# Carrying each answer's destination with its token: the last mixture-of-experts layer of a four-layer graph network

## The chip, the cores and the metric

The kernel runs on one core of a Trainium2 chip. The core has a matrix engine (PE, with its weight loads shown apart as PEld), a vector engine (DVE), an activation engine (ACT), a general engine (POOL, or GpSimd) and a queue engine (SP). DMA transfers are issued from SP, ACT and POOL and are carried by 16 DMA engines that all of them share. Transfers with a list of row numbers (gathers and scatters) are issued from POOL here.

The metric is the device time of one execution in microseconds (us). Before the change it is 6287.54 us, the median of nine runs from 6260.56 to 6317.55 us.

## The reference

3125 nodes with 256 features pass through four layers. Each layer adds a graph layer and a feed-forward layer to x, each applied to a layer norm of x. Only the last feed-forward layer concerns us. It is a mixture of 8 experts of which each token uses the best two:

```python
gate_logits = xf @ Wg + bg
top_w, top_i = jax.lax.top_k(gate_logits, TOP_K)          # TOP_K = 2 of E = 8
top_w = jax.nn.softmax(top_w, axis=-1)
w_dense = jnp.sum(jax.nn.one_hot(top_i, E, dtype=xf.dtype) * top_w[..., None], axis=1)
out = jnp.zeros_like(xf)
for e in range(E):
    h = jax.nn.gelu(xf @ W1[e] + b1[e], approximate=False)  # 256 -> 1024
    out = out + w_dense[:, e:e + 1] * (h @ W2[e] + b2[e])   # 1024 -> 256
```

Then x = x + out, and that is the kernel's output. A token is a node.

## The kernel before

The nodes are kept in an order of the kernel's own, padded to NP = 3200, as NT = 25 tiles of P = 128 rows of D = 256 numbers. X holds all of x in on-chip memory ([128, 25, 256]), XNH holds its layer norm with eight columns to spare ([128, 25, 264]), and XN is the first 256 columns of XNH. `pid(g)` is the list of the nodes' places in the output.

The last feed-forward layer does not compute all experts for all tokens. It sorts the 2 x 3200 choices by expert:

1. *Places* (L1518, `expert_places`). Each choice gets a row, `top_pos`, in a table `top_in` in device memory. The rows of one expert start at a multiple of R3 = 256, so that the table falls into T3 = 32 tiles of 256 rows, each of a single expert. 32 x 256 = 8192 rows hold 6400 choices; the rest stay at zero, which `cleared` (L1503) wrote long before, from the tile `zeros`, while the gates of an earlier layer were computed.
2. *Scatter in.* 50 scatters of 128 rows each (one per node tile and choice, by the helper at L1083) write the normed tokens into `top_in`. They are on POOL.
3. *Turns* (L1575, `in_turns`). For each tile j there are four steps, in a software pipeline written out by hand: in turn s the kernel does `given_back3(s-3)`, `hidden3(s-2)`, `turn_rows3(s-1)` and `load3(s)`, in that order. The order on every engine is the order in which they are written (a manual schedule).
   - `load3` loads the tile's 256 tokens (xq, on ACT's queue) and the weights and biases of the tile's expert (w1, b1, w2, b2, 1 MB each for w1 and w2, on SP's queue).
   - `turn_rows3` transposes the tokens on PE into ft_ps (L2900) and copies them out on DVE (xt, L2901).
   - `hidden3` multiplies by W1 on PE (fh_ps, L2909, 32 matmuls) and applies the GELU on ACT (ht, L2911).
   - `given_back3` multiplies by W2 on PE (fo_ps, L2921, 32 matmuls), adds the bias on DVE (ys, L2923) and writes the 256 answers as a plain block of `top_out`, a table of 8192 rows in the order of `top_in` (L2924, on SP's queue).
4. *The end* (L2928 to L2933). For each of 25 node tiles and each of the two choices, a gather by `top_pos` fetches the answers from `top_out` into y (POOL, helper at L1079, eight buffers), and DVE adds gate times y to X (L2932). A scatter by `pid(g)` then writes X[:, g, :] to the output (POOL, helper at L1083). Rows past the last node are dropped by a bounds check.

The helper `scatter` declares the scatters into one table free of dependences among themselves, because each has rows of its own. Readers of the table wait for the scatters that wrote it.

Of the kernel before, what the change touches and what calls it, by code (L numbers as in the profile page):

```python
# [11 lines left out]
F32 = mybir.dt.float32  # L12
BF16 = mybir.dt.bfloat16
I32 = mybir.dt.int32
AF = mybir.ActivationFunctionType
ALU = mybir.AluOpType
# [4 lines left out]
P = 128  # L21
D = 256
KD = D // P
N = 3125
NT = (N + P - 1) // P
NP = NT * P
# [1029 lines left out]
BATCH = 5  # L1056
# [13 lines left out]
W1 = D + 1  # L1070
# [7 lines left out]
def gather(nc, out_, table, idx):  # L1078
    return nc.gpsimd.indirect_dma_start(out=out_, out_offset=None, in_=table, in_offset=index(idx))  # L1079


def scatter(tc, group, table, idx, in_, **bounds):
    s = tc.nc.gpsimd.indirect_dma_start(out=table, out_offset=index(idx), in_=in_, in_offset=None, **bounds)  # L1083
    tc.declare_no_dep(s.ins, group=group, reason="each node has a row of its own")
    tc.add_to_no_dep_group(group, s.ins)
# [328 lines left out]
def quick(ctx: ExitStack, tc: tile.TileContext, a: dict, out: bass.AP, k):  # L1414
# [3 lines left out]
    nc, dram, ident, ones = tc.nc, k.dram, k.ident, k.ones  # L1418
    q = ctx.enter_context(tc.tile_pool(name="q", bufs=1))
    X = q.tile([P, NT, D], F32, name="X")  # L1420
    XNT = q.tile([P, KD, NP], F32, name="XNT")
    f = parts(tc, a, k, X, XNT)
# [8 lines left out]
    slot = q.tile([P, KS[0]], F32, name="slot")  # L1431
    nc.gpsimd.iota(slot, pattern=[[1, KS[0]]], base=0, channel_multiplier=0,
                   allow_small_or_imprecise_dtypes=True)
    zeros = q.tile([P, D], F32, name="zeros")
    nc.vector.memset(zeros, 0.0)
    zero = zeros[0:1, :]

    def pid(g):
        return PRi[:, g, 0:1]
# [7 lines left out]
    def batches():  # L1447
        return [range(b, b + BATCH) for b in range(0, NT, BATCH)]
# [44 lines left out]
            pass  # L1493


    def token_tables(name, choices, n_exp, rows):


        T = (choices * NP + n_exp * (rows - 1)) // rows
        tin, tout = (dram.tile([T * rows, D], F32, name=f"{name}_{s}") for s in ("in", "out"))  # L1500
        return T, tin, tout

    def cleared(tin):  # L1503

        r = tin.shape[0] // P
        for i in range(0, r, 8):
            n = min(8, r - i)
            nc.sync.dma_start(tin[i * P : (i + n) * P, :].rearrange("(r p) d -> p r d", p=P),
                              zeros[:, None, :].to_broadcast([P, n, D]))
            yield 0  # L1510

    SWE, SWH = 32, 64
    sw_T, sw_in, sw_out = token_tables("sw", 1, SWE, P)
    E3, F3, R3 = 8, 1024, 2 * P
    FC3 = F3 // P
    T3, top_in, top_out = token_tables("top", 2, E3, R3)

    def expert_places(pool, psum, ohs, n_exp, rows, T, pos_i):  # L1518

# [55 lines left out]
    def in_turns(T, steps, beside=None, pace=None):  # L1575


        with tc.manual_schedule():
            for s in range(T + max(d for _, d in steps)):
                for step, d in steps[::-1]:  # L1580
                    if 0 <= s - d < T:
                        step(s - d)
                if beside:
                    for _ in range(pace(s)):
                        next(beside, None)
            if beside:
                for _ in beside:
                    pass
# [127 lines left out]
    for g in range(NT):  # L1716
        w = min(10, P // KS[g])
        n = -(-P // w)
# [11 lines left out]
    with tc.tile_pool(name="ep", bufs=1) as pool:  # L1730
        NJ = max(n for _, n, _ in TILES)
        firsts = pool.tile([P, NT, NJ], F32, name="ep_first")
        for g, (w, _, _) in enumerate(TILES):
            nc.gpsimd.iota(firsts[:, g, :], pattern=[[w, NJ]], base=w, channel_multiplier=0,
                           allow_small_or_imprecise_dtypes=True)
# [4 lines left out]
        t = t_at  # L1740
# [244 lines left out]
    with tc.tile_pool(name="gg", bufs=gbufs) as gp, tc.tile_pool(name="gm", bufs=3) as mp, \  # L1985
# [5 lines left out]
        b2 = f.row(a["L0_gnn_b2"], D, wp, "b2")  # L1991
# [75 lines left out]
    with tc.tile_pool(name="rt", bufs=1) as rt_pool:  # L2067
# [8 lines left out]
        with tc.tile_pool(name="sc", bufs=1) as sc:  # L2076
# [24 lines left out]
            with tc.tile_pool(name="tkp", bufs=1, space=PSUM) as tkp, tc.tile_pool(name="sk", bufs=2) as sk:  # L2101
# [4 lines left out]
                for c0, n in CHUNKS:  # L2106
                    xmt = sk.tile([P, PP, 512], F32, name="xmt")
                    for c in range(PP):
                        ps = tkp.tile([P, 512], F32, name="xm_ps", bufs=2)
# [4 lines left out]
                    for i in range(n // P):  # L2114
                        t = c0 // P + i
# [4 lines left out]
                        sw = SW[:, t, :].rearrange("p (h g) -> p h g", h=H)  # L2120
# [8 lines left out]
                        fx = fxs[t % 2]  # L2129
# [724 lines left out]
    with tc.tile_pool(name="fc", bufs=1) as fc, tc.tile_pool(name="fw", bufs=2) as fw, \  # L2854
            tc.tile_pool(name="fx", bufs=2) as fx, tc.tile_pool(name="fps", bufs=2, space=PSUM) as fps:
        iota_e = f.places(fc, E3)
        ms_, ohs = [], []
        for i in range(2):
            m_ = fc.tile([P, NT], F32, name=f"top{i}")
            nc.vector.tensor_reduce(m_, lg3, AX.X, ALU.max)  # L2860
            o = f.first_of(fc, lg3, m_, iota_e, E3, f"top{i}_oh")
            if i == 0:
                nc.vector.scalar_tensor_tensor(lg3, o, -BIG, lg3, op0=ALU.mult, op1=ALU.add)
            ms_.append(m_)
            ohs.append(o)
        pos = fc.tile([P, 2 * NT], I32, name="top_pos")
        win = expert_places(fc, fps, ohs, E3, R3, T3, pos)
        for i in range(2 * NT):
            scatter(tc, "top_in", top_in, pos[:, i : i + 1], XN[:, i % NT, :])
        gate = fc.tile([P, 2, NT], F32, name="gate")  # L2870
        nc.vector.tensor_sub(gate[:, 1, :], ms_[1], ms_[0])
        nc.scalar.activation(gate[:, 1, :], gate[:, 1, :], AF.Exp)
        nc.vector.tensor_scalar_add(gate[:, 0, :], gate[:, 1, :], 1.0)
        nc.vector.reciprocal(gate[:, 0, :], gate[:, 0, :])
        nc.vector.tensor_mul(gate[:, 1, :], gate[:, 1, :], gate[:, 0, :])
        ld, xt, ht = {}, {}, {}
        regs = {}

        def load3(j):
            if j % WG == 0:  # L2880
                regs["e"] = experts_at(win, j, E3)
            e = bass.ds(regs["e"][j % WG], 1)
            xq = fx.tile([P, 2, D], F32, name="xq")
            nc.scalar.dma_start(xq, top_in[j * R3 : (j + 1) * R3, :].rearrange("(i p) d -> p i d", p=P))
            w1 = fw.tile([P, KD, F3], F32, name="w1")
            nc.sync.dma_start(w1, a["L3_ffn_W1"][e, :, :].rearrange("a (k p) h -> p (a k) h", p=P))
            b1 = fx.tile([P, FC3], F32, name="b1t", bufs=3)
            nc.sync.dma_start(b1, b1t[e, :, :].rearrange("a p f -> p (a f)"))
            w2 = fw.tile([P, FC3, D], F32, name="w2", bufs=3)
            nc.sync.dma_start(w2, a["L3_ffn_W2"][e, :, :].rearrange("a (f p) d -> p (a f) d", p=P))  # L2890
            b2 = fx.tile([P, D], F32, name="b2t", bufs=3)
            nc.sync.dma_start(b2, a["L3_ffn_b2"][e, :].to_broadcast([P, D]))
            ld[j] = xq, w1, b1, w2, b2

        def turn_rows3(j):
            xt[j] = fx.tile([P, KD, R3], F32, name="xt")
            ps = fps.tile([P, KD, R3], F32, name="ft_ps", bufs=1)
            for c in range(KD):
                for i in range(2):
                    nc.tensor.transpose(ps[:, c, i * P : (i + 1) * P], ld[j][0][:, i, c * P : (c + 1) * P], ident)  # L2900
            nc.vector.tensor_copy(xt[j], ps)  # L2901

        def hidden3(j):
            ht[j] = fx.tile([P, FC3, R3], F32, name="ht")
            for f_ in range(0, FC3, 2):
                ps = fps.tile([P, 2, R3], F32, name="fh_ps", bufs=3)
                for i in range(2):
                    for c in range(KD):
                        nc.tensor.matmul(ps[:, i, :], ld[j][1][:, c, (f_ + i) * P : (f_ + i + 1) * P], xt[j][:, c, :],  # L2909
                                         start=(c == 0), stop=(c == KD - 1))  # L2910
                    nc.scalar.activation(ht[j][:, f_ + i, :], ps[:, i, :], AF.Gelu, bias=ld[j][2][:, f_ + i : f_ + i + 1])  # L2911
            xt.pop(j)

        def given_back3(j):
            _, _, _, w2, b2 = ld.pop(j)
            h = ht.pop(j)
            ys = fx.tile([P, 2, D], F32, name="ys")
            ps = fps.tile([P, 2, D], F32, name="fo_ps")
            for i in range(2):
                for f_ in range(FC3):  # L2920
                    nc.tensor.matmul(ps[:, i, :], h[:, f_, i * P : (i + 1) * P], w2[:, f_, :],  # L2921
                                     start=(f_ == 0), stop=(f_ == FC3 - 1))
            nc.vector.tensor_add(ys, ps, b2[:, None, :].to_broadcast([P, 2, D]))  # L2923
            nc.sync.dma_start(top_out[j * R3 : (j + 1) * R3, :].rearrange("(i p) d -> p i d", p=P), ys)  # L2924

        in_turns(T3, ((load3, 0), (turn_rows3, 1), (hidden3, 2), (given_back3, 3)))

        for g in range(NT):  # L2928
            for i in range(2):
                y = fx.tile([P, D], F32, name="y", bufs=8)  # L2930
                gather(nc, y, top_out, pos[:, i * NT + g : i * NT + g + 1])
                nc.vector.scalar_tensor_tensor(X[:, g, :], y, gate[:, i, g : g + 1], X[:, g, :],  # L2932
                                               op0=ALU.mult, op1=ALU.add)  # L2933
            scatter(tc, "out", out, pid(g), X[:, g, :], bounds_check=N - 1, oob_is_err=False)


@with_exitstack
# [60 lines left out]
```

## Time and profile before

The profile shows one execution. Its span, from the first to the last instruction, is 6286.5 us; the execution took 6287.92 us.

| what | number |
|---|---|
| median of nine runs | 6287.54 us |
| the profiled execution, its span | 6287.92 us, 6286.5 us |
| busy over the whole span: PE, DVE, ACT, POOL | 60%, 50%, 19%, 50% |
| granted PE clock over the span (1 is full speed) | 0.758 |
| first and last start of the scatters into `top_in` | 5535.80, 5598.51 us |
| first PE instruction of the expert tiles (ft_ps) | 5603.72 us |
| last ys on DVE (L2923) | 6177.49 us, for 0.69 us |
| first gather of y, last scatter to the output | 6181.49 us, 6277.53 us |
| gathers of y | 50, mean 0.960 us |
| scatters to the output | 25, mean 1.019 us |
| DVE at the end (L2932) | 50, mean 0.484 us |

How to read it: an instruction is named by its line, its engine and out<-in, with the names of the tiles. A line of a helper (L1079 gather, L1083 scatter) appears for many tiles, so the tile's name tells which it is. The idle time before an instruction is put down to what ended it: "<-DMA y" means that the engine waited for a transfer of y, "<-issue" that the profile shows nothing that it waited for. A PE that is busy is not always at full clock; the windows give the granted clock. The chain of waits is followed back from the last instruction, and an engine outside of it may idle at no cost.

### The profile page before, as it was taken

The numbers are of one execution on the slowest core, as the hardware profiler recorded it, in microseconds if no ns is written. First come the engines' busy times: TensorE is split into PE (matmuls) and PEld (weight loads), VectorE is DVE, ScalarE is ACT, GpSimd is POOL, SyncE is SP. The second block draws the span as 40 slices with busy tenths as digits, with TensorE's granted clock in tenths as the row PEclk, the third lists the DMA queues.
The fourth block names the chain that finished last, engine by engine and source line by source line (L and its number), as shares of the span: only waits on it lengthen the run. The fifth ranks groups of instructions, "written<-read, shape, count | busy, mean of one in ns | idle before, by whom it ended". The sixth has DMA issues, their size and how long they took to land. (4 is left out here: it accounts for less than half of the span.)

```text
span 6286.5 us, 45072 instructions
## 1 busy us (share of the span) xinstructions
PE 3784.4 (60%) x14067; PEld 2484.4 (40%) x14119; DVE 3123.7 (50%) x6023; ACT 1222.0 (19%) x2574; POOL 3128.5 (50%) x3044
## 2 busy tenths in 40 slices
PE   2245533455598844535286712889676688838882
PEld 2233332333355423423153411556342344436662
DVE  4578868898874345601153426333224677810001
ACT  1222212445532100000042411110120000012220
POOL 4677774677773266676467573110126566430004
PEclk9667666667799956656598855999656787769996
DMA  4534442333312233222242214332243233234442
GB/s 128 136 96 107 107 109 81 91 92 100 90 23 83 112 91 91 78 74 56 60 147 68 73 38 121 109 110 95 80 117 85 81 88 86 65 109 158 158 159 84
DMA packets 357953, 602.95 MB, mean 96 GB/s; under 512 B 109331, under 2 KB 254331, under 8 KB 354370
## 3 DMA queue, kind: packets, MB, share of 16 engines
q0 software_dynamic: 130800, 329.16, 19.9%
q1 hardware_dynamic: 207657, 251.79, 12.5%
q10 hardware_dynamic: 19238, 18.93, 0.9%
q8 instruction: 116, 1.90, 0.1%
q14 instruction: 142, 1.16, 0.1%
HBM read 458.77 MB, written 142.93 MB: 96 GB/s over the span
## 5 line engine op out<-in xcount | busy, mean ns | idle before, releaser
L1620 PE MATMUL acc<-wv,ident 128*128 128x256 f32 x2818 | 923.6, 488 | 631.7 <-ACT wv L1632 264.8
L1079 POOL DMA_INDIRECT gt<-T,recs x906 | 1013.9, 1119 | 365.2 <-issue 247.7
L1620 PEld LDWEIGHTS acc<-wv,ident 128*128 128x128 f32 x2818 | 662.8, 246 | 893.1 <-ACT wv L1632 297.3
L1079 POOL DMA_INDIRECT gt<-TA,recs x453 | 454.8, 1004 | 259.4 <-issue 127.3
L1079 POOL DMA_INDIRECT gt<-gm,recs x428 | 478.2, 1117 | 180.8 <-issue 128.7
L1079 POOL DMA_INDIRECT gt<-rel,relz x453 | 443.0, 978 | 208.8 <-issue 126.9
L1705 PE MATMUL acc<-gt,ident 128*128 128x256 f32 x906 | 320.0, 485 | 209.1 <-issue 168.2
L2566 PE MATMUL acc<-XNT,adj_g 128*128 128x512 bf16 x1198 | 402.2, 384 | 42.0 <-ACT XNT L2558 42.0
L2797 PE MATMUL e_ps<-EW,att 32*128 32x512 f32 (+7 forms) x466 | 296.7, 764 | 145.8 <-ACT att L2787 106.4
L1672 ACT ACTIVATE m<-m 128x1024 f32<-128x1024 f32 (+2 forms) x258 | 256.5, 994 | 630.7 <-DVE m L1671 370.6
L2569 PE MATMUL acc<-F,adj_g 128*128 128x256 bf16 x1250 | 343.4, 275 | 9.3 <-DVE F L2559 6.6
L1079 POOL DMA_INDIRECT y<-top_out,top_pos x50 | 48.0, 960 | 596.9 <-issue 595.7
L1671 DVE TENSOR_TENSOR m<-gt,R 128x1028 f32<-128x1028 f32 (+4 forms) x258 | 297.0, 1151 | 89.5 <-DMA gt<-T,recs 87.5
L1705 PEld LDWEIGHTS acc<-gt,ident 128*128 128x128 f32 x906 | 205.8, 239 | 303.8 <-issue 196.2
L2909 PE MATMUL fh_ps<-xt,w 128*128 128x256 f32 x1024 | 266.9, 399 | 76.2 <-ACT ht L2911 75.4
L1677 DVE TENSOR_TENSOR m<-m,att 128x1024 f32<-128x1024 f32 (+2 forms) x258 | 294.2, 1140 | 28.0 <-issue 28.0
L1634 DVE TENSOR_TENSOR wv<-gt,L 128x1024 f32<-128x1024 f32 (+3 forms) x252 | 285.2, 1136 | 43.2 <-remote 39.1
L1678 DVE TENSOR_REDUCE L<-m 128x4 f32<-128x1024 f32 (+4 forms) x258 | 294.3, 1141 | 11.2 <-DVE m L1677 3.3
L2438 PE MATMUL x_ps<-XNT,x_w 128*128 128x512 f32 (+1 forms) x448 | 223.6, 633 | 100.8 <-ACT x_h L2440 74.3
L2909 PEld LDWEIGHTS fh_ps<-xt,w 128*128 128x128 f32 x1024 | 187.7, 193 | 150.3 <-ACT ht L2911 128.1
L2459 DVE TENSOR_TENSOR x_y<-x_o,x_b 128x512 f32<-128x512 f32 (+1 forms) x52 | 34.4, 669 | 416.1 <-remote 256.4
L2452 PE MATMUL x_o<-x_w,x_h 128*128 128x256 f32 x800 | 204.7, 401 | 50.4 <-issue 25.7
(557 smaller groups left out, 6603.7 us busy)
## 6 DMA issues: line engine op xcount, KB each, us to landing
w<-in_L_ffn_W_dram SPq DMA_DIRECT2D x64, 1024.0 KB
adj_g<-adj SPq DMA_DIRECT2D x50, 800.0 KB
adj<-em_a SPq DMA_DIRECT2D x25, 800.0 KB
gt<-T,recs POOLq DMA_INDIRECT x906
y<-each_d SPq DMA_DIRECT2D x25, 512.0 KB
each_d<-x_y SPq DMA_DIRECT2D x24, 512.0 KB
R<-rr SPq DMA_DIRECT2D x25, 388.0 KB
top_in<-zeros SPq DMA_DIRECT2D x8, 1024.0 KB
```

Source lines behind the costliest of these rows:

```text
L1079: return nc.gpsimd.indirect_dma_start(out=out_, out_offset=None, in_=table, in_offset=index(idx))
L1620: nc.tensor.matmul(acc, ident, wv[:, s, :], start=(c + s == 0), stop=(c + s == K - 1))
L1634: nc.vector.tensor_mul(wv[:, :n, :].rearrange("p s (h c) -> p s h c", h=H), t[:, :n, :D].rearrange("p s (h c) -> p s h c", h=H), L[:, c : ...
L1671: nc.vector.tensor_add(m[:, :n, :], st[g].tiles[c][:, :n, :], st[g].R[:, 1:2, :].to_broadcast([P, n, W]))
L1672: nc.scalar.activation(m[:, :n, :D], m[:, :n, :D], AF.Abs)
L1677: nc.vector.tensor_mul(m[:, :n, :D], m[:, :n, :D], att[:, None, :].to_broadcast([P, n, D]))
L1678: nc.vector.tensor_reduce(L, m[:, :n, :D].rearrange("p s (h c) -> p s h c", h=H), AX.X, ALU.add)
L1705: nc.tensor.matmul(accs[g], ident, t[:, s, :], start=False, stop=(last and s == n - 1))
L2566: nc.tensor.matmul(acc.rearrange("p s d -> p (s d)"), A[:, b, :], F12[:, b, :, :].rearrange("p s d -> p (s d)"), start=(b == 0), stop=Fals ...
L2569: nc.tensor.matmul(acc[:, 0, :], A[:, b, :], F3_[:, b, :], start=False, stop=(b == NT - 1), skip_group_check=True)
L2797: nc.tensor.matmul(e_ps[:, :z, :].rearrange("p s d -> p (s d)"), att, EW[: att.shape[0], s0 : s0 + z, :].rearrange("p s d -> p (s d)"), st ...
L2909: nc.tensor.matmul(ps[:, i, :], ld[j][1][:, c, (f_ + i) * P : (f_ + i + 1) * P], xt[j][:, c, :], start=(c == 0), stop=(c == KD - 1))
```

## The change

`top_out` becomes a table in the order of the nodes: row n for the first choice of node n, row 3200 + n for its second, 6400 rows in all. Each token carries the row of its answer with it:

- Rows of `top_in` have 257 numbers instead of 256; the last is the destination less 8192 (OUTSIDE). `zeros` and the clearing writes are 257 wide as well, so that a row that holds no token has a zero there, hence the destination 8192, which is past the table's end.
- The column behind XN in XNH is set to the row of the first choice (an iota on POOL, a copy on DVE). After each of the first 25 scatters into `top_in` DVE sets it to the row of the second choice for that tile, which it can do only when the scatter has read it.
- xq is 257 wide. After the copy xt, DVE turns the last column into the integers `to` ([128, 2] for a tile).
- `given_back3` no longer writes `top_out`. Two new steps of the turn, `send(0)` and `send(1)`, scatter the two halves of ys to `top_out` by `to`, with a bounds check that drops the destination 8192. Each is followed on POOL by a memset of a one-number tile, `mark`. ys has three buffers instead of two.
- The end has no gathers. For each of five batches of five node tiles, two plain loads of 640 KB (one on SP's queue with the first choice's rows, one on ACT's with the second's) bring the answers into y, with two buffers. The 50 DVE operations and the 25 scatters to the output stay.

```diff
--- before.py
+++ after.py
@@ -1431,9 +1431,9 @@
     slot = q.tile([P, KS[0]], F32, name="slot")
     nc.gpsimd.iota(slot, pattern=[[1, KS[0]]], base=0, channel_multiplier=0,
                    allow_small_or_imprecise_dtypes=True)
-    zeros = q.tile([P, D], F32, name="zeros")
+    zeros = q.tile([P, W1], F32, name="zeros")
     nc.vector.memset(zeros, 0.0)
-    zero = zeros[0:1, :]
+    zero = zeros[0:1, :D]
 
     def pid(g):
         return PRi[:, g, 0:1]
@@ -1493,12 +1493,11 @@
             pass
 
 
-    def token_tables(name, choices, n_exp, rows):
+    def token_table(name, choices, n_exp, rows, width):
 
 
         T = (choices * NP + n_exp * (rows - 1)) // rows
-        tin, tout = (dram.tile([T * rows, D], F32, name=f"{name}_{s}") for s in ("in", "out"))
-        return T, tin, tout
+        return T, dram.tile([T * rows, width], F32, name=name)
 
     def cleared(tin):
 
@@ -1506,14 +1505,18 @@
         for i in range(0, r, 8):
             n = min(8, r - i)
             nc.sync.dma_start(tin[i * P : (i + n) * P, :].rearrange("(r p) d -> p r d", p=P),
-                              zeros[:, None, :].to_broadcast([P, n, D]))
+                              zeros[:, None, : tin.shape[1]].to_broadcast([P, n, tin.shape[1]]))
             yield 0
 
     SWE, SWH = 32, 64
-    sw_T, sw_in, sw_out = token_tables("sw", 1, SWE, P)
+    sw_T, sw_in = token_table("sw_in", 1, SWE, P, D)
+    sw_out = dram.tile([sw_T * P, D], F32, name="sw_out")
     E3, F3, R3 = 8, 1024, 2 * P
     FC3 = F3 // P
-    T3, top_in, top_out = token_tables("top", 2, E3, R3)
+
+    OUTSIDE = 8192
+    T3, top_in = token_table("top_in", 2, E3, R3, W1)
+    top_out = dram.tile([2 * NP, D], F32, name="top_out")
 
     def expert_places(pool, psum, ohs, n_exp, rows, T, pos_i):
 
@@ -2865,22 +2868,29 @@
             ohs.append(o)
         pos = fc.tile([P, 2 * NT], I32, name="top_pos")
         win = expert_places(fc, fps, ohs, E3, R3, T3, pos)
+        node = fc.tile([P, NT], F32, name="node")
+        nc.gpsimd.iota(node, pattern=[[P, NT]], base=-OUTSIDE, channel_multiplier=1,
+                       allow_small_or_imprecise_dtypes=True)
+        nc.vector.tensor_copy(XNH[:, :, D], node)
         for i in range(2 * NT):
-            scatter(tc, "top_in", top_in, pos[:, i : i + 1], XN[:, i % NT, :])
+            g = i % NT
+            scatter(tc, "top_in", top_in, pos[:, i : i + 1], XNH[:, g, :W1])
+            if i < NT:
+                nc.vector.tensor_scalar_add(XNH[:, g, D:W1], node[:, g : g + 1], float(NP))
         gate = fc.tile([P, 2, NT], F32, name="gate")
         nc.vector.tensor_sub(gate[:, 1, :], ms_[1], ms_[0])
         nc.scalar.activation(gate[:, 1, :], gate[:, 1, :], AF.Exp)
         nc.vector.tensor_scalar_add(gate[:, 0, :], gate[:, 1, :], 1.0)
         nc.vector.reciprocal(gate[:, 0, :], gate[:, 0, :])
         nc.vector.tensor_mul(gate[:, 1, :], gate[:, 1, :], gate[:, 0, :])
-        ld, xt, ht = {}, {}, {}
+        ld, xt, ht, ys, to = {}, {}, {}, {}, {}
         regs = {}
 
         def load3(j):
             if j % WG == 0:
                 regs["e"] = experts_at(win, j, E3)
             e = bass.ds(regs["e"][j % WG], 1)
-            xq = fx.tile([P, 2, D], F32, name="xq")
+            xq = fx.tile([P, 2, W1], F32, name="xq")
             nc.scalar.dma_start(xq, top_in[j * R3 : (j + 1) * R3, :].rearrange("(i p) d -> p i d", p=P))
             w1 = fw.tile([P, KD, F3], F32, name="w1")
             nc.sync.dma_start(w1, a["L3_ffn_W1"][e, :, :].rearrange("a (k p) h -> p (a k) h", p=P))
@@ -2899,6 +2909,8 @@
                 for i in range(2):
                     nc.tensor.transpose(ps[:, c, i * P : (i + 1) * P], ld[j][0][:, i, c * P : (c + 1) * P], ident)
             nc.vector.tensor_copy(xt[j], ps)
+            to[j] = fx.tile([P, 2], I32, name="to", bufs=4)
+            nc.vector.tensor_scalar(to[j], ld[j][0][:, :, D], float(OUTSIDE), None, op0=ALU.add)
 
         def hidden3(j):
             ht[j] = fx.tile([P, FC3, R3], F32, name="ht")
@@ -2914,24 +2926,34 @@
         def given_back3(j):
             _, _, _, w2, b2 = ld.pop(j)
             h = ht.pop(j)
-            ys = fx.tile([P, 2, D], F32, name="ys")
+            ys[j] = fx.tile([P, 2, D], F32, name="ys", bufs=3)
             ps = fps.tile([P, 2, D], F32, name="fo_ps")
             for i in range(2):
                 for f_ in range(FC3):
                     nc.tensor.matmul(ps[:, i, :], h[:, f_, i * P : (i + 1) * P], w2[:, f_, :],
                                      start=(f_ == 0), stop=(f_ == FC3 - 1))
-            nc.vector.tensor_add(ys, ps, b2[:, None, :].to_broadcast([P, 2, D]))
-            nc.sync.dma_start(top_out[j * R3 : (j + 1) * R3, :].rearrange("(i p) d -> p i d", p=P), ys)
-
-        in_turns(T3, ((load3, 0), (turn_rows3, 1), (hidden3, 2), (given_back3, 3)))
-
-        for g in range(NT):
-            for i in range(2):
-                y = fx.tile([P, D], F32, name="y", bufs=8)
-                gather(nc, y, top_out, pos[:, i * NT + g : i * NT + g + 1])
-                nc.vector.scalar_tensor_tensor(X[:, g, :], y, gate[:, i, g : g + 1], X[:, g, :],
-                                               op0=ALU.mult, op1=ALU.add)
-            scatter(tc, "out", out, pid(g), X[:, g, :], bounds_check=N - 1, oob_is_err=False)
+            nc.vector.tensor_add(ys[j], ps, b2[:, None, :].to_broadcast([P, 2, D]))
+
+        def send(i):
+            def step(j):
+                scatter(tc, "top_out", top_out, to[j][:, i : i + 1], ys[j][:, i, :],
+                        bounds_check=2 * NP - 1, oob_is_err=False)
+                nc.gpsimd.memset(mark, 0.0)
+            return step
+
+        mark = fc.tile([1, 1], F32, name="mark")
+        in_turns(T3, ((load3, 0), (turn_rows3, 1), (hidden3, 2), (send(1), 3), (send(0), 3), (given_back3, 3)))
+
+        for b, gs in enumerate(batches()):
+            y = fx.tile([P, 2, BATCH, D], F32, name="y", bufs=2)
+            for i, engine in enumerate((nc.sync, nc.scalar)):
+                r = i * NP + gs[0] * P
+                engine.dma_start(y[:, i, :, :], top_out[r : r + BATCH * P, :].rearrange("(t p) d -> p t d", p=P))
+            for g in gs:
+                for i in range(2):
+                    nc.vector.scalar_tensor_tensor(X[:, g, :], y[:, i, g - gs[0], :], gate[:, i, g : g + 1],
+                                                   X[:, g, :], op0=ALU.mult, op1=ALU.add)
+                scatter(tc, "out", out, pid(g), X[:, g, :], bounds_check=N - 1, oob_is_err=False)
 
 
 @with_exitstack
```

## The prediction

> **What bounds the kernel now.** I read the page's chain first, by line: fh_ps and fo_ps, the experts' matmuls, hold 4% of the span each, and the new places (top_in 1%, y 1%) little. So I went to the windows of the last stages, then to the tile top_out, then to the timeline of the end. Windows, columns: length, busy time (and count) of PE, its weight loads, DVE, ACT, POOL; granted clock, DMA share, GB/s.
>
> ```profile
> 5700.00:5800.00 100.00, 86.14 (x382) 68.18 (x381) 7.61 (x11) 22.30 (x47) 0.00 (x0) 1.00 0.45 151
> 6200.00:6250.00 50.00, 0.00 (x0) 0.00 (x0) 12.54 (x27) 0.00 (x0) 38.12 (x40) 0.50 0.33 102
> ```
>
> The experts' stage is PE's: 86 us of 100 at a granted clock of 1.00, POOL with nothing at all, DVE 8%, DMA at under half. A tile takes 17.63 us there. The end is POOL's, with 40 DMAs in 50 us, DVE a quarter busy and DMA a third.
>
> The tile top_out shows who lives on it (us, times):
>
> ```profile
> L1079 POOL DMA_INDIRECT y<-top_out,top_pos x50: 945/956/981, 6181.5 to 6273.9; - x50
> L2924 SPq DMA_DIRECT2D top_out<-ys x32: 360/372/372, 5631.9 to 6178.2; - x32
> ...
>   POOL y L1079: 582.0, 1
>   DVE X L2932: 73.4, 48
> ```
>
> POOL sleeps 582 us through the experts; then DVE waits 73.4 us for gathers. The timeline (start, duration, engine, instruction, idle before) gives both ends of that stretch:
>
> ```profile
> 6177.49 0.69 DVE L2923 TENSOR_TENSOR ys<-fo_ps,b2t 128x512 f32<-128x512 f32 x1 [16.50 <-PE fo_ps L2921]
> 6178.21 0.36 SPq L2924 DMA_DIRECT2D top_out<-ys  x1
> 6181.49 0.98 POOL L1079 DMA_INDIRECT y<-top_out,top_pos  x1 [582.02 <-issue]
> ...
> 6276.77 0.48 DVE L2932 SCALAR_TENSOR_TENSOR X<-y,gate,X 128x256 f32<-128x256 f32 x1 [2.23 <-DMA y<-top_out,top_pos]
> 6277.53 1.00 POOL L1083 DMA_INDIRECT out_dram<-X,PR  x1 [1.33 <-DVE X L2932]
> ```
>
> From the last ys (6177.49) to the span's end (6286.5) are 109 us; 96 of them are 75 POOL DMAs, 50 gathers and 25 scatters, one every 1.28 to 1.32 us. The last starts 8.97 us before the end.
>
> **The change part by part.** The sum is made against the profiled execution: 6287.92 us, a span of 6286.5 and 1.42 around it. The median of the nine runs is 6287.54, 0.4 below it; they reach from 6260.56 to 6317.55. About 0.3% (19 us) is what a measurement of this kernel can tell from no change.
>
> *Rows of 257 numbers in top_in.* The eight clearing writes grow by 0.4%, in a stage where SP writes them beside the gates' matmuls. Of the 50 scatters (0.975 each at a pitch of 1.28, 5535.80 to 5598.51) the nearest wide row is T<-r,PR of 257 numbers: 0.971 at least, 0.988 in the median, against 0.975. So 0.013 x 50 = 0.7 us, on the path, for the first xq load waits for the last scatter (5598.51, +2.25 landed, xq at 5600.98, first matmul 5603.72). Bounds: -0.2 by the shortest row, 11 by the longest (1.202). I take 0.7. The xq loads grow by 0.4% and come a turn ahead; only the first is bare (2.55 us, so +0.01).
>
> *Destinations.* The iota is one POOL instruction (0.16 for such a one at 5510), while POOL waits 24.7 us for top_pos; the copy into XNH is one of DVE's small ones there, in a gap of 1.9 us. The 25 additions (128x1) go after scatter g and wait for its landing, 2.25 us; scatter 25+g, which needs it, starts 25 x 1.28 = 32 us after scatter g. Behind them on DVE stand only the gate's few operations and xt, first needed at 5604.87, while the last addition is done by about 5535.8 + 24 x 1.28 + 3 = 5570. Zero; without that cover 25 x 2.5 = 62 us.
>
> *In the experts' turns.* One more DVE operation per tile (to, 128x2) behind the xt copy, in an engine that is 92% idle. It waits for the scatters that read its buffer four tiles before, sent two turns (35 us) ago; behind it stand the next ys and xt. The plain write to top_out leaves SP (0.36 of its queue, and its wait for ys with it, so b2's load now carries that wait itself; w1, b1, w2, b2 keep their order). On POOL, empty here, come two scatters and two one-number memsets, 2 x 1.28 + 2 x 0.1 = 2.8 us of 17.63. The bytes are the same 256 KB, in DMA engines that are 45 to 50% busy. PE's order of matmuls does not change. Zero; bounds: -0.5 per tile if SP's freed queue brings weights sooner (PE is idle 13%; fh_ps's row puts 75.4 of its 76.2 us of idle time to ACT's ht, which it would not touch, so I take none of it), and up to 1 per tile if software packets delay the weights.
>
> *Handover.* The last ys is done at 6178.18. A POOL DMA follows DVE 0.28 later (6276.77 + 0.48 to 6277.53): scatter 0 at 6178.5, memset, scatter 1 at about 6179.9. A plain load behind a scatter, and what follows it, has its like in another stage: the F<-gcn loads, 640 KB each and of the same tile shape.
>
> ```profile
> 3939.16 0.98 POOL L1083 DMA_INDIRECT gcn<-own,PR  x1 [0.31 <-issue]
> 3941.60 0.93 SPq L2556 DMA_DIRECT2D F<-gcn  x2
> 3946.18 1.26 ACT L2558 CAST XNT<-F 128x1280 bf16<-128x1280 f32 x1 [22.64 <-DMA F<-gcn]
> 3948.02 2.42 ACT L2558 CAST XNT<-F 128x1280 bf16<-128x1280 f32 x2 [0.58 <-DMA F<-gcn]
> ```
>
> Load 2.44 after the last scatter, data of the first 4.58 later, of the second 6.42 later, 1.84 for each further one. So the y loads go out at 6182.3, batch 0 (two of them) is there at 6188.8, batch 1 at 6192.4.
>
> *The end.* DVE has 50 operations: 0.40 each where such ones run back to back (13 in 5.24 with y<-each_d), so 4.1 for a batch of ten. Batches 0 and 1 run 6188.8 to 6197.0; batch 2 needs batch 0's buffer (free at 6192.9, loaded 6.42 later): 6199.4; batch 3 follows to 6207.6; batch 4 needs batch 2's buffer: 6209.9 to 6214.0. POOL has 25 scatters of 1.02 + 0.30 = 1.32. If DVE did not touch them: first at 6190.0, last 24 x 1.32 later at 6221.7, end 8.97 later at 6230.6.
>
> But DVE may. One scatter of the GCN layer ran while DVE went through additions with both inputs in SBUF (X<-X,b and X<-X,XN, without a gap from 3910.11 to 3923.95):
>
> ```profile
> 3912.20 12.60 POOL L1083 DMA_INDIRECT gcn<-own,PR  x1 [1.48 <-ACT XNT L1487]
> ...
> 3923.19 0.76 DVE L2629 TENSOR_TENSOR X<-X,XN 128x256 f32<-128x256 f32 x2
> ```
>
> and the window 3915 to 3920:
>
> ```profile
> 3915.00:3920.00 5.00, 4.61 (x27) 3.82 (x26) 5.00 (x16) 3.36 (x9) 5.00 (x1) 1.00 0.00 0
> ```
>
> It took 12.60 instead of 1.27, the DMA engines moved nothing, and it ended 0.85 after DVE's train. The end's operation (X<-y,gate,X) has both inputs in SBUF too, at 0.40 instead of 0.335. Before, each stands alone, begins over 0.12 into a gather and does not lengthen it (0.945 to 0.981). After, they come in trains of 8.2, 8.2 and 4.1. Held like that one, the first scatter (6189.7) ends at 6197.9, a second fits into the gap, the third is held to 6208.4, a fourth fits, the fifth is held to 6214.9; the other 20 start from 6215.1, the last at 6215.1 + 19 x 1.32 = 6240.2. End 6249.2. The bounds for the hold are thus 0 and 18.6 us. I take the full hold: that row is nearest (same engine pair, both inputs in SBUF, operations of 0.3 to 0.4 back to back), while the unheld gathers had no train over them.
>
> The Trainium skill, SBUF — State Buffer, section Who interferes with whom, says that a DVE instruction with two SBUF inputs contends with GpSimd's reads through a shared port, held for a whole instruction, but infers that tensor_tensor does not stall descriptor generation. By that inference the end is at 6230.6; the 12.60 row speaks against it, and no row here shows the three-input operation in a train.
>
> *Sum.* End 6249.2 + 0.7 for top_in + 1.42 around the span - 0.4 to the median = 6250.9, say 6250: 37 less, 0.6%.
>
> **The rivals.**
> *No hold* (the above without it): 6230.6 + 0.7 + 1.0 = 6232. For it: 50 unheld gathers before; against it: the 12.60 row. A hold in part, if scatters slip in between two of DVE's operations, lies between the two.
> *The handover or the loads cost more.* If y's 6.5 MB come at the 98 GB/s of before's end rather than at some 350 GB/s, they take 67 us and end the kernel at 6182.3 + 67 + 4.1 + 5 x 1.32 + 8.97 = 6269. For it: the DMA engines write out beside them; against it: F<-gcn, with 384 GB/s in the window 3944 to 3946. With this, 6258 to 6285.
> *Slower: the scatters in the experts' turns hold up PE.* Place: DVE's to and ys wait for POOL's scatters of earlier tiles, and xt, which PE needs, stands behind them. It decides over the gain when each tile loses over 37/32 = 1.2 us, which asks that a scatter lasts beyond the two turns of room, some 35 us, or that weights come that much late by DMA contention. For it: 64 software DMAs beside 2 MB of weights per tile; against it: DMA at half, DVE at 8%, and its only train-like partner (ys and xt) has one input in PSUM. At 2 us per tile: 6250 + 64 = 6314.
>
> **How the numbers follow.** Full hold 0.48 (6240 to 6262), no or small hold 0.28 (6225 to 6240), dearer loads 0.13, slower experts 0.11. The range 6222 to 6270 holds the first two and half of the third. Faster by over 0.3% (under 6269): 0.48 + 0.28 + 0.06 = 0.82; slower 0.11; the same 0.07.
>
> **What would show it.** Right: the experts' tile still at 17.6 us; 64 scatters of about 1 us on POOL there; y loads issued 4 to 5 us after the last ys; in the end, out scatters of 4 to 9 us while DVE works and then a row of about 20 at 1.32. All scatters at 1.0 from the first on means no hold. Wrong: PE's busy share falling below 86% between 5700 and 6170, a first matmul later than 5606, or y loads over 10 us.

## The result

The changed kernel takes 6223.99 us (median of ten runs, 6188.21 to 6253.98) against 6287.54 (31 runs by then). The ratio of the two sets of runs is 0.9903, 95% interval 0.9882 to 0.9925, so 61 us less (47 to 74). The forecast was 6250 with a range of 6222 to 6270. The direction and the place were right, but the median lies only 2 us above the lower edge of the range, and it is nearer to the rival without a hold (6232) than to the case that was taken for the likeliest. What had to be found out below is why the scatters were held so little.

The profiled execution has a span of 6236.0 us, 50.5 less than before. The views of the changed kernel that answer to those of the prediction are first the windows of the experts' stage and of the end (length; busy time and count of PE, weight loads, DVE, ACT, POOL; granted clock, DMA share, GB/s):

```profile
5700.00:5800.00 100.00, 87.28 (x388) 69.86 (x388) 8.74 (x18) 20.45 (x44) 12.77 (x24) 1.00 0.50 164
6200.00:6225.00 25.00, 0.00 (x0) 0.00 (x0) 13.43 (x33) 0.00 (x0) 19.62 (x18) 0.50 0.75 254
```

The experts' stage is PE's as before; POOL now has 13 us of 100 in it, beside PE. In the end the DMA engines are at 0.75, where they were at 0.33, and POOL has 18 instructions in 25 us. Then the tile top_out (us, times):

```profile
L1083 POOL DMA_INDIRECT top_out<-ys,to x64: 983/986/997, 5637.9 to 6184.7; - x64
L2951 SPq DMA_DIRECT2D y<-top_out x5: 359/360/526, 6186.8 to 6209.0; - x5
L2951 ACTq DMA_DIRECT2D y<-top_out x5: 457/458/552, 6186.9 to 6209.0; - x5
...
  DVE X L2954: 15.5, 6
```

64 scatters of at most 0.997 us, none of them held, and DVE waits 15.5 us for y where it waited 73.4. And the timeline of the end (start, duration, engine, instruction, idle before):

```profile
6182.47 0.69 DVE L2935 TENSOR_TENSOR ys<-fo_ps,b2t 128x512 f32<-128x512 f32 x1 [16.50 <-PE fo_ps L2933]
...
6184.73 0.99 POOL L1083 DMA_INDIRECT top_out<-ys,to  x1 [0.24 <-issue]
...
6186.85 22.47 SPq L2951 DMA_DIRECT2D y<-top_out  x5
...
6192.52 3.87 DVE L2954 SCALAR_TENSOR_TENSOR X<-y,gate,X 128x256 f32<-128x256 f32 x9 [9.36 <-DMA y<-top_out]
6194.29 0.98 POOL L1083 DMA_INDIRECT out_dram<-X,PR  x1 [8.49 <-DVE X L2954]
6195.58 1.27 POOL L1083 DMA_INDIRECT out_dram<-X,PR  x1 [0.30 <-issue]
...
6200.19 1.68 POOL L1083 DMA_INDIRECT out_dram<-X,PR  x1 [0.30 <-DVE X L2954]
6202.17 0.99 POOL L1083 DMA_INDIRECT out_dram<-X,PR  x1 [0.30 <-issue]
...
6227.86 0.99 POOL L1083 DMA_INDIRECT out_dram<-X,PR  x1 [0.30 <-issue]
```

From the start of the last ys to the end of the span there are now 53.5 us instead of 109.0: 55.5 less. Of the 25 scatters the longest takes 1.68 us although DVE works beside them in trains, rows of up to eleven operations without a gap. From the first to the last they take 33.57 us; 24 steps of 0.99 + 0.30 would be 30.96, so DVE costs them 2.6 us here.

What comes ahead of the end differs by 5 us between the two executions. The scatters into top_in, the first step that the change touches on the path, start 8.9 us later in the profile of after (5544.7 against 5535.8). Of this 4.8 us are there at the clearing writes of sw_in (3003.2 against 2998.4), ahead of every clearing write that became wider; that the rest has nothing to do with the change is likely, but not shown. The first expert tile takes 23.1 us from the start of its xt to the end of its ys where it took 27.0; a second profile of the changed kernel has 27.0 there as well.

### The profile page after: what moved, and what is told of

Its sections match the earlier page's. It is cut to its first block, busy times and chain, and to the rows that moved or that the text cites. A ratio compares the mean times of both kernels' runs of the same rounds, so it can differ in the third digit from the quotient of the medians.

```text
span 6236.0 us, 45320 instructions
## 1 busy us (share of the span) xinstructions
PE 3777.2 (61%) x14067; PEld 2480.2 (40%) x14119; DVE 3126.6 (50%) x6081; ACT 1222.0 (20%) x2574; POOL 3147.7 (50%) x3123
## 3 DMA queue, kind: packets, MB, share of 16 engines
q1 hardware_dynamic: 202233, 246.71, 12.5%
## 5 line engine op out<-in xcount | busy, mean ns | idle before, releaser
L1083 POOL DMA_INDIRECT top_out<-ys,to x64 | 63.1, 986 | 509.6 <-DVE ys L2935 455.9
L1681 DVE TENSOR_REDUCE L<-m 128x4 f32<-128x1024 f32 (+4 forms) x258 | 294.3, 1141 | 15.5 <-remote 5.5
L2810 DVE SCALAR_TENSOR_TENSOR m<-e_ps,XN 128x512 f32<-128x512 f32 (+1 forms) x233 | 149.2, 669 | 158.4 <-remote 62.4
L2933 PE MATMUL fo_ps<-w,ht 128*128 128x256 f32 x1024 | 226.3, 379 | 0.0
```

Of the source, the lines that this page charges most:

```text
L1681: nc.vector.tensor_reduce(L, m[:, :n, :D].rearrange("p s (h c) -> p s h c", h=H), AX.X, ALU.add)
```

## The experiments

The runs fell on three chips, on which the kernel before takes 6287.5, 5853 to 5854 and 6213.5 us. So whole times are compared only on one chip, and stages by their own length in the trace. "The end" is from the start of the last ys to the end of the span. All kernels are the changed kernel with the edit shown. Those that try the kind of operation, the constant, the order of the inputs and the bounds check were timed once each, so they are read by their stages alone.

**The gathers put back.** Is the gain that of the end's gathers alone?

```diff
-            for i, engine in enumerate((nc.sync, nc.scalar)):
-                engine.dma_start(y[:, i, :, :], top_out[r : r + BATCH * P, :].rearrange(...))
+        nc.gpsimd.iota(at, pattern=[[P, 2 * NT]], base=0, channel_multiplier=1)
...
+                gather(nc, y, top_out, at[:, i * NT + g : i * NT + g + 1])
```

> The changed kernel whose end gathers again, 50 times 128 rows by a list on POOL, but from the table in the order of the nodes; the carried destinations and the 64 scatters in the experts' turns stay. If the gain is the end's 50 gathers, the stretch from the last ys to the end goes back from 53.5 us to about 109 (75 POOL DMAs at 1.28 to 1.32, 8 to 9 behind the last) and the kernel to that of before, 6280 to 6290 us; the experts' tile stays at 17.63. If part of the gain comes from the experts' stage without the write on SP, the kernel stays faster than before by that part, 4 us or more.

Measured: 5854.32 us against 5853.04 of the kernel before, ratio 0.9996 (0.9979 to 1.0012). The end is 105.6 us (5741.50 to 5847.1), from the tile top_out and the timeline:

```profile
L1079 POOL DMA_INDIRECT y<-top_out,at x50: 942/956/992, 5746.1 to 5838.4; - x50
...
  DVE X L2953: 75.3, 50
```

With the gathers back the whole gain is gone, with the wider rows, the 25 additions, the 64 scatters and the memsets all in place. So all these together cost or bring nothing that can be measured (the interval reaches 0.2%, some 12 us, to either side), and the experts' stage without its write on SP takes the 546.0 us of the changed kernel. The end is 3.4 us shorter than the 109.0 of before because 5.1 us instead of 9.0 lie behind the start of its last scatter; why is open. The first expert tile took 23.4 us here, and 27.0 in a second profile of the unaltered changed kernel on this chip: its 3.9 us are no part of the change.

**What lets a scatter in: the kind of operation?** The prediction took the one gcn scatter of 12.60 us for the like of the end. First, the end's operation was made the GCN layer's, then its constant operand was tried, and then the GCN layer's train was made the end's.

```diff
-  nc.vector.scalar_tensor_tensor(X[:, g, :], y[:, i, g - gs[0], :], gate[:, i, g : g + 1], X[:, g, :], ...)
+  nc.vector.tensor_add(X[:, g, :], y[:, i, g - gs[0], :], X[:, g, :])
```

> In the end each of DVE's 50 operations is a plain addition of y to X (tensor_tensor) in place of gate times y plus X; the gates are left out of the result. Theory K (the kind of operation decides: POOL gets no chance between two tensor_tensors with both inputs in SBUF, but does between two scalar_tensor_tensors): the first scatters are held over a train of ten or more, 3 to 8 us each, as the one of 12.7 us in the GCN layer; the stretch from the last ys to the end grows from 53.5 to 60 to 68 us. Theory P (the place decides: what held the GCN layer's scatter was something else there, such as its rows or PE and ACT at work beside it): scatters of 1.0 to 1.7 us as now, 52 to 54 us.

Measured: the end is 52.2 us. The timeline of the end shows additions at 0.335 us a piece (seven in 2.50) and scatters beside them of at most 1.23:

```profile
5762.15 2.50 DVE L2954 TENSOR_TENSOR X<-y,X 128x256 f32<-128x256 f32 x7 [0.30 <-DMA y<-top_out]
5762.85 0.98 POOL L1083 DMA_INDIRECT out_dram<-X,PR  x1 [8.73 <-DVE X L2954]
5764.14 1.03 POOL L1083 DMA_INDIRECT out_dram<-X,PR  x1 [0.30 <-DVE X L2954]
5765.04 3.78 DVE L2954 TENSOR_TENSOR X<-y,X 128x256 f32<-128x256 f32 x11 [0.39 <-DMA y<-top_out]
5765.47 1.18 POOL L1083 DMA_INDIRECT out_dram<-X,PR  x1 [0.30 <-DVE X L2954]
5766.96 1.04 POOL L1083 DMA_INDIRECT out_dram<-X,PR  x1 [0.30 <-DVE X L2954]
```

```diff
-  ... y[:, i, g - gs[0], :], gate[:, i, g : g + 1], X[:, g, :], ...
+  ... y[:, i, g - gs[0], :], 0.5, X[:, g, :], ...
```

> In the end each of DVE's 50 operations multiplies y by the constant 0.5 in place of the gate read from SBUF; the gates are left out of the result. If the operand read from SBUF is what lets POOL in between two operations, scatters are now held over trains, 3 to 8 us each, and the stretch from the last ys to the end is 60 to 68 us. If the kind of operation is (theory K) or the place (theory P), nothing changes: scatters of 1.0 to 1.7 us, 52 to 54 us.

Measured: the end is 52.4 us, scatters of at most 1.25:

```profile
L1083 POOL DMA_INDIRECT out_dram<-X,PR x25: 983/993/1250, 5756.9 to 5789.3; - x25
```

```diff
-  nc.vector.tensor_add(X[:, g, :], X[:, g, :], b2)
-  nc.vector.tensor_add(X[:, g, :], X[:, g, :], XN[:, g, :])
+  nc.vector.scalar_tensor_tensor(X[:, g, :], X[:, g, :], 1.0, b2, op0=ALU.mult, op1=ALU.add)
+  nc.vector.scalar_tensor_tensor(X[:, g, :], X[:, g, :], 1.0, XN[:, g, :], op0=ALU.mult, op1=ALU.add)
```

> In the GCN layer the two tensor_tensors of the train, X plus bias and X plus XN, become scalar_tensor_tensors of the same tiles (X times 1.0 plus the other), in the same order; the end is that of the changed kernel. Theory K: the one gcn scatter of 12.7 us goes down to under 2 us, while DVE's train is a little longer (40 operations at 0.40 instead of 0.335). Theory P: it stays at 12 us or more. The kernel's time stays within 0.3% by both, since that scatter has slack or is worth 10 us at most.

Measured: one gcn scatter of 14.42 us. The tile's row (min, median, max of the duration in ns; first and last start):

```profile
L1083 POOL DMA_INDIRECT gcn<-own,PR x50: 967/976/14418, 3609.0 to 3909.3; - x50
```

Theory K falls in both directions. The same additions that hold a scatter for 12 us in the GCN layer hold none in the end for more than 0.25 us, and the end's kind of operation holds one for 13 us in the GCN layer.

**Is it DVE's train at all?** The GCN layer's additions were left out.

```diff
-  nc.vector.tensor_add(X[:, g, :], X[:, g, :], b2)
-  nc.vector.tensor_add(X[:, g, :], X[:, g, :], XN[:, g, :])
```

> In the GCN layer the 50 additions of DVE's train (X plus bias, X plus XN) are left out, so the result lacks them; the rest is the changed kernel. If DVE's train is what holds the one gcn scatter, the scatter goes down from 12.7 us to 1.0 to 1.3, the scatters behind it and the F loads come some 11 us sooner, and the kernel is 5 to 12 us faster than the changed one. If the scatter is held by something else, it stays at 12 us or more and the kernel's time stays.

Measured: the longest gcn scatter takes 1.178 us, and the F loads start 37.6 us after the first gcn scatter (3825.7 to 3863.3) instead of the 45.6 to 49.5 of the kernels that have the additions there:

```profile
L1083 POOL DMA_INDIRECT gcn<-own,PR x50: 966/974/1178, 3825.7 to 4116.2; - x50
L2559 SPq DMA_DIRECT2D F<-gcn x10: 359/360/527, 3863.3 to 4139.5; - x10
```

So DVE's train is what holds that scatter, and it costs the layer 8 to 12 us, before and after the change alike. The time was 6146.91 us, 0.991 (0.9883 to 0.9938) of the kernel before on that chip. The changed kernel is at 0.9903 on another chip, so the whole time does not show the expected gain of 5 to 12 us; the stage does.

**The order of the inputs?** In the end X is the second input, in the GCN layer the first. Both were turned round.

```diff
-  nc.vector.tensor_add(X[:, g, :], X[:, g, :], b2)
+  nc.vector.tensor_add(X[:, g, :], b2, X[:, g, :])
-  nc.vector.tensor_add(X[:, g, :], X[:, g, :], XN[:, g, :])
+  nc.vector.tensor_add(X[:, g, :], XN[:, g, :], X[:, g, :])
```

> In the GCN layer the same additions have their two inputs in the other order: b plus X and XN plus X, so that X is the second input, as in the end of the changed kernel. If which tile is the second input decides whether POOL gets in between two operations, the gcn scatter goes down from 12.7 us to under 2. If not, it stays at 12 us or more.

Measured: 11.227 us at most. The order does not free the scatter.

```profile
L1083 POOL DMA_INDIRECT gcn<-own,PR x50: 967/974/11227, 3847.5 to 4150.4; - x50
```

```diff
-  nc.vector.scalar_tensor_tensor(X[:, g, :], y[:, i, g - gs[0], :], gate[:, i, g : g + 1], X[:, g, :], ...)
+  nc.vector.tensor_add(X[:, g, :], X[:, g, :], y[:, i, g - gs[0], :])
```

> In the end each of DVE's operations is the addition of X and y in this order, X the first and y the second input, as in the GCN layer's train (the gates are left out). If the order of the inputs decides, scatters to the output are held over trains now, 3 to 8 us each, and the stretch from the last ys to the end grows from 53.5 us to 60 to 68. If not, it stays at 52 to 54, with scatters of 1.0 to 1.3 us.

Measured: scatters of at most 1.252 us, an end of 51.3. The order does not hold them either.

```profile
L1083 POOL DMA_INDIRECT out_dram<-X,PR x25: 984/987/1252, 6083.3 to 6115.0; - x25
```

**The bounds check?** The scatters to the output have one, those of the GCN layer none.

```diff
-  scatter(tc, "gcn0", tables[0], pid(g), own[:, g, :])
+  scatter(tc, "gcn0", tables[0], pid(g), own[:, g, :], bounds_check=NP - 1, oob_is_err=False)
```

> The scatters into the first GCN table get a bounds check as the scatters to the output have it; nothing is dropped by it. If the check is what lets a scatter in between two of DVE's operations, the one of 12.7 us goes down to under 2 us and the stretch to the first F load to 37 to 39 us. If not, it stays at 11 us or more.

Measured: 14.087 us at most, 47.3 us to the first F load. It is not the check.

```profile
L1083 POOL DMA_INDIRECT gcn<-own,PR x50: 965/993/14087, 3608.2 to 3908.1; - x50
```

**The GCN layer's additions moved.** What the held scatter costs can be had back.

```diff
-  nc.vector.tensor_add(X[:, g, :], X[:, g, :], b2)
-  nc.vector.tensor_add(X[:, g, :], X[:, g, :], XN[:, g, :])
   nc.vector.scalar_tensor_tensor(X[:, g, :], acc, dinv[:, g : g + 1], X[:, g, :], op0=ALU.mult, op1=ALU.add)
+  nc.vector.tensor_add(X[:, g, :], X[:, g, :], b2)
+  nc.vector.tensor_add(X[:, g, :], X[:, g, :], XN[:, g, :])
```

> The changed kernel once more, on the same chip as the next two: 0.988 to 0.9925 of the kernel before by the first measurement; by the stages of the trace 52 to 56 us less at the end and 0 to 4 at the first expert tile.

> The changed kernel with the GCN layer's two additions (X plus bias, X plus XN) moved behind the operation that needs the neighbours' sum, so that they can't be done ahead while the gcn scatters run. If DVE's train is what held the one scatter and nothing else takes its place, the stretch from the first gcn scatter to the first F load goes down from 46 to 49 us to 37 to 39, and the kernel is 7 to 11 us faster than the changed one (0.1 to 0.2%). If the additions cost in their new place what they saved, it is the same within 3 us.

Measured on one chip: the changed kernel 5804.52 us, 0.9909 (0.9894 to 0.9925) of the kernel before; with the additions moved 5796.74, 0.9897 (0.9880 to 0.9913). The tile gcn in the changed kernel and, in the second fence, with the additions moved:

```profile
L1083 POOL DMA_INDIRECT gcn<-own,PR x50: 967/974/12847, 3611.9 to 3910.2; - x50
L2559 SPq DMA_DIRECT2D F<-gcn x10: 359/360/527, 3657.5 to 3934.3; - x10
```

```profile
L1083 POOL DMA_INDIRECT gcn<-own,PR x50: 967/971/1167, 3609.5 to 3898.6; - x50
L2559 SPq DMA_DIRECT2D F<-gcn x10: 359/360/528, 3644.2 to 3922.6; - x10
```

The held scatter is gone. The stretch to the first F load falls from 45.6 to 34.7 us, and the stretch from there to the next layer's first scatter (sw_in) grows from 523.1 to 527.0, where the additions now stand: 7 us less by the stages, 7.8 by the medians. The intervals of the two kernels overlap, so the whole time alone does not show it; the first stage does. Whether the second one grew by the additions is not shown, since it takes 522.9 to 526.6 us in the kernels that left them where they were.

**No list at the end.** If the 25 scatters at 1.29 us bound the new end, writing in output order should shorten it.

```diff
-            scatter(tc, "top_in", top_in, pos[:, i : i + 1], XNH[:, g, :W1])
+            scatter(tc, "top_in", top_in, pos[:, i : i + 1], XNH[:, g, : W1 + 1])
...
+        for g in range(NT):
+            scatter(tc, "x_out", x_out, pid(g), X[:, g, :])
...
+                nc.vector.tensor_scalar(ys[j][:, i, :], ys[j][:, i, :], gq[j][:, i : i + 1], None, op0=ALU.mult)
...
-                scatter(tc, "out", out, pid(g), X[:, g, :], bounds_check=N - 1, oob_is_err=False)
+            nc.scalar.dma_start(out[r : r + n * P, :].rearrange("(t p) d -> p t d", p=P), xs[:, :n, :])
```

> A further step along the change: the carried destination is the node's place in the output, and the gate is carried as well (rows of 258 numbers; ys is multiplied by it in the experts' turns). X is scattered into output order while the experts compute (25 scatters on POOL, then five plain loads of 640 KB on SP), so that the end has no list at all: ten plain loads of y on SP, ten additions of 128x1280 on DVE, six plain stores on ACT's queue. If the 25 scatters at 1.29 us are what bounds the changed kernel's end, the stretch from the last ys to the end goes down from 53.5 us to 33 to 42 (9.8 MB at 300 to 380 GB/s and 6 to 8 us of handover and last store), and the kernel is 10 to 20 us faster than the changed one, 0.2 to 0.35%. If the 9.8 MB of loads and stores bound the end already, or if the 25 scatters and loads of X hold up the experts, it gains under 5 us or loses.

> Both steps, the output order at the end and the later additions in the GCN layer. By the stages of the two single kernels 12 us less at the end (40.4 against 52.8) and 10 in the GCN layer: 18 to 24 us faster than the changed kernel, 0.3 to 0.4%, so 0.985 to 0.988 of the kernel before. If the rows of 258 numbers, the scatter of X or its five loads cost the experts what the end gains, the gain is 10 us or less.

Measured: the end is 41.1 us in the first and 42.1 in the second, as expected, but the kernels are not faster than the changed one: 6171.51 us, 0.9950 (0.9923 to 0.9977) of the kernel before on its chip, and with the GCN step, on the chip of the last two, 5807.16, 0.9913 (0.9898 to 0.9928). What the end gained was lost earlier. The tile x_out of the second one:

```profile
L1083 POOL DMA_INDIRECT x_out<-X,PR x25: 970/992/1917, 4571.6 to 5106.7; - x25
L2948 SPq DMA_DIRECT2D X<-x_out x5: 372/492/610, 5321.8 to 5392.5; - x5
```

The expectation placed these 25 scatters into the experts' turns. They are not there (the first xt of that kernel is at 5197.7). They stand outside the order written out by hand, and each was put where its row tile of X became ready: among the gathers of the last graph layer, where POOL is busy for 155.8 us of 200 (4805 to 5005) with 146 instructions, most of them 0.30 us apart, which about fills the time. That layer, from the first load of sw_in's tokens to the first scatter into top_in, takes 921.4 us in this kernel and 890.5 to 901.2 in the seven others profiled on this chip. The excess is some 20 to 31 us. The 25 DMAs of POOL, 28.0 us busy in that stage, would add 35.5 us at 1.12 + 0.3 us each if nothing hid them. That they are the cause is argued from this, and no run shows it alone. The granted clock hardly differs (0.81 and 0.84 in two windows; 0.86 and 0.85 with the additions moved alone, 0.85 and 0.83 in the changed kernel). The same scatters written into the experts' turns by hand were not tried.

## Why the prediction was right, and where not

*What bounds what.* Right. The experts' tile takes 17.63 us before and after, the 32 of them 546.4 and 546.0 from the first ys to the last, with 64 scatters beside them; the end was the place of the gain, as the kernel with gathers shows.

*The front.* Right. The 50 wider scatters take 62.6 us from the first to the last start (5544.7 to 5607.3) against 62.7, with the additions in between; 0.7 had been put in. The rival of a slower experts' stage was not seen. Two small slips change nothing: the row of the iota reads 0.15 us and not 0.16, and the first scatter to the output starts at 6190.0 in one sum and at 6189.7 in the other.

*The handover.* Right within 1.3 us: loads 4.4 us after the start of the last ys (4.8 forecast), DVE's first operation 10.05 after it (11.3), the first scatter 11.8 (12.5 without a hold).

*The hold.* This is the term that was mis-sized: "I take the full hold". It was put at 18.6 us and measured 2.6; in the seven profiled kernels with this same end it is 2.5 to 4.1. That is 16 of the 18 us between the forecast end, 71.7 us from the last ys, and the measured 53.5. The prediction's own working without a hold ends 53.1 us after the last ys. That this comes so near to 53.5 is in part luck: a first scatter 0.7 us earlier, a pitch of 1.29 instead of 1.32 (0.7 in all) and 0.8 us less behind the last scatter nearly make up for the 2.6.

The reading that chose the full hold went by likeness of two rows: same pair of engines, both inputs in SBUF, short operations without gaps. The mechanism is there (without DVE's additions the gcn scatter falls from 12.7 to 1.2 us), but likeness did not carry it to the end. The trace of before could have shown that the row is an exception: of its 2893 POOL transfers with a list, 559 take over 1.05 us, and the longest but this one takes 3.87.

In the end a scatter caught by DVE gets in when the running operation ends, or else it waits until the train stops. The ten profiled kernels that scatter to the output from such trains have 250 of these scatters. Of them 104 take over 1.00 us, and each of the 104 ends 0.86 us, within 0.03, behind the end of a DVE operation. For 94 it is the operation that had begun last when the scatter started (1.28 us at most), and in 78 of these cases the next operation follows without a gap. For the other ten it is the last operation of the train, one to three later (1.67 to 2.47 us); the 1.68 in the lines above is one of them. So the assumption that every scatter waits for the end of its train is what failed; "a hold in part, if scatters slip in between two of DVE's operations", named with the rival, is what came.

What decides whether a scatter gets in is not settled. The kind of operation, an operand read from SBUF, the order of the inputs and the bounds check are excluded, each by a run. What stands beside the train, such as PE and ACT, which work through it in the GCN layer and rest in the end, was not tried. But the place alone can't decide: in the GCN layer too one scatter goes through in the same train that holds the next. The second profile of the changed kernel shows it (DVE's additions run from 3626.07 to 3639.89 without a gap):

```profile
3626.07 0.41 DVE L2632 TENSOR_TENSOR X<-X,XN 128x256 f32<-128x256 f32 x1
3626.35 0.98 POOL L1083 DMA_INDIRECT gcn<-own,PR  x1 [0.30 <-ACT own L2592]
3627.90 12.85 POOL L1083 DMA_INDIRECT gcn<-own,PR  x1 [0.57 <-ACT XNT L1487]
...
3639.15 0.74 DVE L2632 TENSOR_TENSOR X<-X,XN 128x256 f32<-128x256 f32 x2
```

PE and ACT were at work beside the first of the two as well (1.61 and 1.36 of the 2 us from 3626). A scatter that does not get in pays for the rest of its train: 30 to 40 operations in the GCN layer, three at most in the end. Why none in the end missed its chance earlier in a train is open.

The Trainium skill, SBUF — State Buffer, section Who interferes with whom, infers that a tensor_tensor does not stall descriptor generation. The end nearly agrees (52.2 us with 50 of them, scatters at most 0.25 us longer); the gcn scatter, which falls from 12.7 to 1.2 us when 50 of them are left out, does not.

*The loads.* The rival of dear loads did not come: the DMA engines moved 254 GB/s from 6200 to 6225 beside the scatters.

*The chances.* "No or small hold" had 0.28 and was the case that came, against 0.48 for the full hold. The measured median lies 8 us below that case's 6232 and 1 us below the 6225 at which its band begins; that it is inside the whole range is by a margin of 2 us. The traces' 55.5 us lie on 6232, and the two measurements of the ratio, 0.9903 and 0.9909, differ from 6232 over 6287.54 (0.9912) by less than their intervals.

## What to carry to other kernels

Where one row shows a large price and 50 others none, price both and look how often the trace pays the large one, before taking it for the rule; here that choice was worth 16 us of 55. Work on an idle engine beside a bound one was free here (64 scatters beside PE), but only if it is really put there: 25 scatters meant for the experts' stage went to where their inputs were ready, a stage in which POOL has no time left, and the gain of 12 us at the end was lost there. After a bound is removed, look at the stages one by one: a gain of 7 us in one of them shows in its length while the whole time is still within the noise.

## What the runs showed of the hardware

Some 40 of DVE's additions of two tiles in SBUF in a row (13.8 us at 0.335 each) made one POOL scatter of the GCN layer take 11.2 to 14.4 us in each of the eleven profiled kernels that had them, or their like, ahead; in the profile of before no byte moved meanwhile (3915 to 3920). With the additions moved or left out, the longest scatter took 1.09 to 1.18. The same train let the scatter just ahead through in 0.98 to 0.99 us in three of these kernels. In the kernel's end such operations at the same pace of 0.335 us made a scatter 0.27 us longer at most, and trains of gate times y plus X, at 0.396, up to 1.48 us longer. There 94 of 104 caught scatters got in at the end of the running operation, and ten waited until the train stopped. What decides between the two stays unexplained.
